# Attention heads of a graph network: small VectorE work given to ScalarE and GpSimd, and the causal mask added in the eviction

## The chip, the cores and the metric

The kernel is one program on one core of one Trainium2 chip. The metric is the device time of an execution in microseconds, lower is better; the number quoted is the median of several executions.

## What is computed

Two layers on 3327 nodes of 256 features. Layer 0 is a graph convolution and a mixture of experts, layer 1 a graph attention and then a causal multi-head attention with four query "experts" for each of four heads. Only that last part, the heads, is touched. The reference, cut to it (x is first layer-normalised):

```python
sx = einsum('bsh,ndh->bnsd', x, hl_w) + hl_b          # 4 heads of 64
pad = sx == 0
q = einsum('bnsd,neod->bneso', sx, wq)                # 4 experts a head
k = einsum('bnsd,nod->bnso', sx, wk)
v = einsum('bnsd,nod->bnso', sx, wv)
scores = einsum('bnesd,bntd->bnest', q, k) * d ** 0.5 + causal   # 0 or -inf above the diagonal
att = softmax(scores)
qkv = where(pad, 0, einsum('bnest,bntd->bnesd', att, v))
gs = softmax(out @ gate_w + gate_b)                   # out: qkv, experts side by side
hn = layernorm(sum over experts of qkv * gs + sx)     # over 64, with gain and bias
fx = hn, heads side by side;  pm = fx == 0
hx = relu(where(pm, 0, fx @ fc1 + fc1_b))
hx = layernorm(where(pm, 0, hx @ fc2 + fc2_b) + fx)
out = hx * softmax(hx @ fgate_w) by head              # added to x
```

## The kernel before

The rows stand in 26 tiles of 128. `heads` (L869) works through 104 units, a unit being one tile t and one head h (L1363), and each unit's keys are cut into t // 4 + 1 chunks of up to 512 (`span`, L1008); there are 392 chunks (L1364). For one chunk there are these steps:

- `fill` (L1015): TensorE makes the scores of the four experts, two products at a time in the upper and the lower half of the rows, into four PSUM banks. In the last chunk of a unit (`last`) each bank gets two more bf16 products, `own` times `after` (L1030 to L1036), that add -1e30 above the diagonal: eight products in all.
- `drain` (L1038): VectorE evicts each of the four banks to `sc` in SBUF with one instruction that also takes the row maximum into `mx` (L1046). After the last chunk the maxima are reduced to `nmax`.
- `weigh` (L1058): ScalarE takes Exp of the four parts with the maximum as bias and adds up the row sums.
- `turn` (L1079): VectorE transposes the weights in blocks of 32 x 32, in place.
- `attend` (L1091): TensorE multiplies the turned weights by the values `vr` into `po`.
- `over` (L1110) and `back` (L1120), once a unit: ScalarE copies `po` to `ot`, GpSimd multiplies it by the pad mask `sxd`, TensorE turns it back with the gate products (`ptO`), ScalarE copies that out.

Beside these run two kinds of generators, which do one step each time `run` (L1000) is called. `prepare` (L916), one for each tile, normalises the rows of the next tile, makes `sxt` (the sx of the reference, transposed), values, keys and queries; `sxd` is `sxt` in another layout, loaded by four DMAs on SP's queue, and compared with zero on VectorE (L994). `tail` (L1185), one for each tile but the last, does all from the gate softmax to the output, with `softmax4` (L1148) and `norm4` (L1166). The last tile has its own `last_tail` (L1262).

The order on each engine is the order of the program: `InOrder` (L50) chains each engine's instructions, so an engine that waits holds all behind it. The main loop (L1411 to L1433) drains some chunks ahead (`wanted`, L1397: all of a unit's maxima must be there before its first Exp), attends chunk k, turns chunk k + 1, asks for the values of chunk k + 2 on SP, does half of its Exp, calls `back` and `over` where a unit ended, gives the generators one step (after tile 7 not in the chunk that follows a unit's end, L1426), does the other half of Exp, and fills the next chunk. All products but `po` share one pool of four PSUM banks (`ps`, L881), score chunks and small work alike. `empty` (L892) sends an eviction to ScalarE or VectorE, whichever has the smaller sum in `load`; the amounts added to `load` are the author's costs. The constants of this stage are loaded and made by `heads_fixed` (L777) during the graph stage before it.

Nearly all instructions show line L61 in the profile, that of the recording helper, so groups are told apart by the names of their tiles.

Of the kernel before, what the change touches and what calls it, by code (L numbers as in the profile page):

```python
# [12 lines left out]
F32 = mybir.dt.float32  # L13
# [88 lines left out]
class Net:  # L102
# [674 lines left out]
    def heads_fixed(self, one, nc):  # L777


        a = self.a  # L780

        def load(src, shape, name):
            t = one.tile(shape, F32, name=name)
            nc.sync.dma_start(out=t, in_=src)
            return t

        def load_rows(src, n, name):
            return load(src.partition_broadcast(P), [P, n], name)
# [53 lines left out]
        own = [one.tile([P, P], BF16, name=f"own{k}") for k in range(2)]  # L842
        after = [one.tile([P, P], BF16, name=f"after{k}") for k in range(2)]

        def where(t, op, base, sign=1):

            for k in range(2):
                r = t[ds(64 * k, 64), :]
                nc.gpsimd.affine_select(
                    out=r, in_=r, compare_op=op, fill=0.0, base=base,  # L850
                    pattern=[[sign, P]], channel_multiplier=-2 * sign,
                )

        for k in range(2):
            yield
            nc.gpsimd.memset(own[k], 1.0)
            nc.gpsimd.memset(after[k], NEG)
        for made in (
            (own[0], ALU.is_ge, 0), (own[0], ALU.is_ge, 1, -1), (after[0], ALU.is_ge, -2),
            (own[1], ALU.is_equal, 0), (after[1], ALU.is_equal, -1),  # L860
        ):
            yield
            where(*made)
        self.fixed = (
            hlt, hlb, wv, gb, lng, lnb, fc1, fb1, fc2, fb2, fng, fnb, fgw, wk, wq, igw, own, after
        )


    def heads(self, xs, vs, out):  # L869
# [3 lines left out]
        with ExitStack() as ctx:  # L873
# [9 lines left out]
            hlt, hlb, wv, gb, lng, lnb, fc1, fb1, fc2, fb2, fng, fnb, fgw, wk, wq, igw, own, after = (  # L883
# [28 lines left out]

            def prepare(t, res):  # L916
# [10 lines left out]
                nc.gpsimd.tensor_tensor(rs, rs, self.nhalf[:, :1], ALU.pow)  # L927
                load["dve"] += 0.7
                yield
                xn = self.work.tile([P, D], F32, tag="xn", name="xn2", bufs=1)  # L930
                nc.vector.tensor_scalar(xn, x, mv[:, 0:1], rs, ALU.subtract, ALU.mult)
                load["dve"] += 0.35
# [11 lines left out]
                for c in range(2):  # L944
                    nc.scalar.activation(
                        sxt[:, c, :], pp[:, c, :], AF.Identity, bias=hlb[:, c : c + 1]
                    )
                load["act"] += 0.6
# [3 lines left out]
                for k in range(2):  # L952
                    for s in range(2):
                        nc.sync.dma_start(
                            out=sxd[ds(64 * k, 64), s::2, :], in_=sxt[ds(64 * s, 64), :, :]
                        )
# [37 lines left out]
                nc.vector.tensor_scalar(sxd, sxd, 0.0, None, ALU.not_equal)  # L994
                load["dve"] += 0.4
# [19 lines left out]
            def fill(u, g):  # L1015
# [4 lines left out]
                last = g == t // 4  # L1020
                pq = u["pq"] = []
                for i in range(2):
                    pq += [ps.tile([P, BLK], F32, tag="b", name="pqk") for _ in range(2)]
                    for k in range(2):
# [3 lines left out]
                            start=True, stop=not last,  # L1028
                        )
                    for m in range(2 if last else 0):  # L1030
                        for k in range(2):
                            r = ds(64 * k, 64)
                            nc.tensor.matmul(
                                pq[2 * i + k][:, n - P : n], own[m][r, :], after[m][r, :],
                                start=False, stop=(m == 1),
                            )  # L1036

            def drain(u, g):  # L1038

                n = span(u["t"], g)[1] * P  # L1040
                if g == 0:
# [3 lines left out]
                for e in range(4):  # L1045
                    nc.vector.tensor_scalar(  # L1046
                        sc[:, e, :n], u["pq"][e][:, :n], 1.0, None,
                        ALU.mult, ALU.max, accum_out=u["mx"][:, e, g : g + 1],
                    )
                    load["dve"] += 0.12 + 0.00104 * n  # L1050
                if g == u["t"] // 4:
# [6 lines left out]
            def weigh(u, g, experts):  # L1058
# [3 lines left out]
                if u["h"] == g == 0 and 0 in experts:  # L1062
                    q["den"] = sm.tile([P, 16, 7], F32, tag="den", name="aden", bufs=3)
# [15 lines left out]
            def turn(u, g):  # L1079
# [5 lines left out]
                load["dve"] += 0.1 + 0.00417 * n  # L1085

# [33 lines left out]
            def back(u):  # L1120
# [4 lines left out]
                if h == 0:  # L1125
                    r["qkv"] = tl.tile([P, 4, 4, 64], F32, tag="qkv", name="qkv", bufs=2)
                    r["glp"] = sm.tile([P, 4, 4, 4], F32, tag="glp", name="glp")
# [20 lines left out]
            def softmax4(g, n, tag):  # L1148
# [12 lines left out]
                nc.vector.tensor_tensor(s3, s3, m.unsqueeze(2).to_broadcast([P, n, 4]), ALU.mult)  # L1161
                load["dve"] += 0.6
# [3 lines left out]
            def norm4(v, g, b, tag):  # L1166

                mv = sm.tile([P, 4, 2], F32, tag=tag + "mv", name=tag + "mv")
                for h in range(4):
                    st = sm.tile([P, 6], F32, tag=tag + "st", name=tag + "st")  # L1170
                    nc.vector.bn_stats(st, v[:, ts(h, 64)])
                    nc.vector.bn_aggr(mv[:, h, :], st)
                rs = sm.tile([P, 4], F32, tag=tag + "rs", name=tag + "rs")
                nc.vector.tensor_scalar(
                    rs, mv.rearrange("p h s -> p s h")[:, 1, :], 1e-8, None, ALU.add
                )
                load["dve"] += 1.1
                nc.gpsimd.tensor_tensor(rs, rs, self.nhalf[:, :4], ALU.pow)
                v3 = v.rearrange("p (h d) -> p h d", h=4)
                nc.gpsimd.tensor_tensor(v3, v3, mv[:, :, 0:1].to_broadcast([P, 4, 64]), ALU.subtract)  # L1180
# [4 lines left out]
            def tail(t, sx, qkv, glp, den):  # L1185
# [16 lines left out]
                nc.vector.tensor_tensor(gs, gs, rd, ALU.mult)  # L1202
# [13 lines left out]
                norm4(fx, lng, lnb, "l1")  # L1216
# [3 lines left out]
                turned(fx, fxt)  # L1220
                yield
                h1 = tl.tile([P, 2, P], F32, tag="h1", name="h1")
# [6 lines left out]
                nc.vector.scalar_tensor_tensor(h1, fxt, 0.0, h1, ALU.not_equal, ALU.mult)  # L1229
                load["dve"] += 0.4  # L1230
                yield
                p2 = ps.tile([P, D], F32, tag="b", name="ph2")
                for c in range(2):
                    nc.tensor.matmul(p2[:, ts(c, P)], h1[:, c, :], fc2, start=True, stop=True)
                fo = tl.tile([P, D], F32, tag="fo", name="fo", bufs=3)
                nc.vector.tensor_tensor(
                    fo.rearrange("p (h d) -> p h d", h=4),
                    p2.rearrange("p (h d) -> p h d", h=4), rows(fb2), ALU.add,
                )
                nc.vector.scalar_tensor_tensor(fo, fx, 0.0, fo, ALU.not_equal, ALU.mult)  # L1240
                load["dve"] += 0.8
# [3 lines left out]
                norm4(fo, fng, fnb, "l2")  # L1245
# [4 lines left out]
                x = tl.tile([P, D], F32, tag="xend", name="xend", bufs=2)  # L1250
# [11 lines left out]
            def last_tail(t, c, sx, r):  # L1262
# [4 lines left out]
                if c == 0:  # L1267
# [3 lines left out]
                    x = r["x"] = tl.tile([P, D], F32, tag="xend", name="xend", bufs=2)  # L1271
# [45 lines left out]
                gs = yield from softmax4(gl, 2, "lgs")  # L1317
# [17 lines left out]
                h1 = tl.tile([P, P], F32, tag="h1", name="h1")  # L1335
# [21 lines left out]
                fg = yield from softmax4(pg, 1, "fg")  # L1357
# [632 lines left out]
```

## Time and profile before

| | us |
|---|---|
| median of three runs | 3050.26 |
| lowest, highest | 3046.64, 3051.62 |
| the profiled execution | 3033.66 |
| its span, first to last instruction | 3032.0 |
| first score product (start of the heads) | about 985 |
| VectorE busy in the span | 2506.5 |
| TensorE busy in the span | 2702.8 |
| ScalarE busy in the span | 1678.2 |
| GpSimd busy in the span | 886.5 |

The profile is one execution. A group's row gives the engine, the operation, output and input tiles with their shapes, the count, then the busy time and the mean duration, then the time the engine idled just before these instructions and what ended it. Matmul durations overlap and their ends are modelled. In a table of stretches the columns are span, then busy time (and number of instructions) of TensorE, its weight loads, VectorE, ScalarE and GpSimd, then the granted TensorE clock, the DMA share and GB/s. In a list of waits a row says who waited for whom: total, times and longest.

### The profile page before, as it was taken

The numbers are of one execution on the slowest core, as the hardware profiler recorded it, in microseconds if no ns is written. First come the engines' busy times: TensorE is split into PE (matmuls) and PEld (weight loads), VectorE is DVE, ScalarE is ACT, GpSimd is POOL, SyncE is SP. The second block draws the span as 40 slices with busy tenths as digits, with TensorE's granted clock in tenths as the row PEclk, the third lists the DMA queues.
The fourth block names the chain that finished last, engine by engine and source line by source line (L and its number), as shares of the span: only waits on it lengthen the run. The fifth ranks groups of instructions, "written<-read, shape, count | busy, mean of one in ns | idle before, by whom it ended". The sixth has DMA issues, their size and how long they took to land.

```text
span 3032.0 us, 126726 instructions
## 1 busy us (share of the span) xinstructions
PE 2702.8 (89%) x54254; PEld 2004.2 (66%) x54254; DVE 2506.5 (83%) x6203; ACT 1678.2 (55%) x4570; POOL 886.5 (29%) x1178
## 2 busy tenths in 40 slices
PE   7999988788899789998999998899989999999885
PEld 6878877667677666666666666666656666666554
DVE  5103643789997689999999999999999999999996
ACT  6410144555554556565666665666656666566664
POOL 6441644711322254432332221222121111111121
PEclk9999999889999889999999999999999999999998
DMA  9994578567773223333333343333333433433332
GB/s 376 356 314 134 190 240 261 199 212 253 247 266 99 67 74 110 95 95 104 111 99 106 104 120 105 99 111 105 111 107 104 116 107 114 116 111 106 113 106 74
DMA packets 258194, 449.81 MB, mean 148 GB/s; under 512 B 58816, under 2 KB 156608, under 8 KB 257504
## 3 DMA queue, kind: packets, MB, share of 16 engines
q1 hardware_dynamic: 245536, 417.50, 44.6%
q0 software_dynamic: 6576, 18.02, 1.6%
q8 instruction: 428, 7.01, 1.0%
q10 hardware_dynamic: 5520, 6.18, 0.6%
q14 instruction: 134, 1.10, 0.1%
HBM read 393.37 MB, written 25.88 MB: 138 GB/s over the span
## 4 chain that ended last, share of the span: by engine, by line
DVE 48%; PE 19%; issue 2%; ACT 1%; DMA 0%; POOL 0%; SPq 0%; DVEq 0%; POOLq 0%; ACTq 0%
DVE sc L61 40%; PE po L61 7%; PE pqk L61 6%; PE acc L61 2%; PE ptO L61 1%; DVE fo L61 1%; DVE l2mv L61 1%; DVE l1mv L61 1%; ACT sc L61 0%; PE pq L61 0%; DVE anmax L61 0%; DVE gl L61 0%; DVE l2st L61 0%; PE psxt L61 0%; DVE l1st L61 0%
## 5 line engine op out<-in xcount | busy, mean ns | idle before, releaser
L61 ACT ACTIVATE sc<-sc,anmax 128x512 f32<-128x512 f32 (+3 forms) x1568 | 1041.1, 670 | 124.1 <-DVE anmax L61 123.9
L61 DVE TENSOR_SCALAR_CACHE_REDUCE sc<-pqk 128x512 f32<-128x512 f32 (+3 forms) x1568 | 897.9, 626 | 52.8 <-PE pqk L61 50.9
L61 PEld LDWEIGHTS po<-sc,vr 32*64 32x64 f32 x43728 | 666.0, 131 | 337.7 <-DVE sc L61 195.5
L61 PE MATMUL po<-sc,vr 32*64 32x128 f32 x43728 | 769.2, 276 | 117.2 <-DVE sc L61 74.2
L61 PE MATMUL pqk<-kt,qt 64*128 64x512 f32 (+3 forms) x3136 | 800.4, 581 | 44.6 <-DVE sc L61 17.1
L61 DVE STREAM_TRANSPOSE sc<-sc 128x2048 f32<-128x2048 f32 (+3 forms) x392 | 816.1, 2082 | 12.9 <-ACT sc L61 12.9
L61 PEld LDWEIGHTS pqk<-kt,qt 64*128 64x128 f32 x3136 | 314.4, 187 | 232.4 <-issue 80.0
L61 PE MATMUL acc<-wh,p 128*128 128x259 f32 x1352 | 310.0, 387 | 34.6 <-DVE p L61 34.5
L61 PEld LDWEIGHTS acc<-wh,p 128*128 128x128 f32 x1352 | 254.2, 191 | 92.7 <-DVE p L61 51.9
L61 PE MATMUL acc<-y,pan 128*128 128x256 f32 x1352 | 301.3, 382 | 11.9 <-DMA pan<-in_adjt_dram 10.2
L61 POOL TENSOR_TENSOR ot<-ot,sxd 128x512 f32<-128x512 f32 x103 | 131.7, 1279 | 611.1 <-ACT ot L61 600.8
L61 ACT ACTIVATION_READ_ACCUMULATOR sc<-sc,anmax 128x1 f32 x1568 | 302.1, 193 | 0.0
L61 PEld LDWEIGHTS acc<-y,pan 128*128 128x128 f32 x1352 | 256.0, 191 | 52.2 <-issue 17.5
L61 ACT ACTIVATE u<-u,d 128x512 f32<-128x512 f32 (+1 forms) x182 | 125.1, 688 | 159.5 <-DVE u L61 159.3
L61 ACT COPY qkv<-ptO 128x256 f32<-128x256 f32 x104 | 38.7, 373 | 222.9 <-PE ptO L61 222.9
L61 DVE SCALAR_TENSOR_TENSOR u<-bc,d 128x512 f32<-128x512 f32 (+1 forms) x182 | 135.8, 747 | 0.1
L61 DVE SCALAR_TENSOR_TENSOR p<-pan,u 128x512 f32<-128x512 f32 (+1 forms) x182 | 126.4, 694 | 10.0 <-PE acc L61 5.7
L61 PE MATMUL ptO<-igw,ot 128*128 128x68 f32 x832 | 116.4, 284 | 15.6 <-DVE sc L61 11.6
L61 DVE DVE_READ_ACCUMULATOR sc<-pqk 128x1 f32 x1568 | 128.6, 82 | 0.0
L61 PEld LDWEIGHTS ptO<-igw,ot 128*128 128x128 f32 x832 | 102.3, 193 | 34.8 <-issue 20.9
L61 ACT ACTIVATE junk<-ar 128x1664 bf16<-128x1664 f32 x52 | 82.7, 1591 | 66.7 <-DMA ar<-in_adj_dram 65.4
L61 PEld LDWEIGHTS <-own 64*128 64x128 bf16 x832 | 53.7, 95 | 94.5 <-issue 82.9
(324 smaller groups left out, 2872.5 us busy)
## 6 DMA issues: line engine op xcount, KB each, us to landing
vr<-vs SPq DMA_DIRECT2D x976, 128.0 KB, 2.6
ar<-in_adj_dram SPq DMA_DIRECT2D x104, 832.0 KB, 7.8
vr<-vs SPq DMA_DIRECT2D x544, 96.0 KB, 2.2
pan<-in_adjt_dram SPq DMA_DIRECT2D x156, 256.0 KB, 4.7
pan<-in_adjt_dram SPq DMA_DIRECT2D x26, 1024.0 KB, 10.7
pan<-in_adjt_dram SPq DMA_DIRECT2D x20, 832.0 KB, 4.7
w1e<-w SPq DMA_DIRECT2D x59, 256.0 KB, 2.5
took<-places SPq DMA_DIRECT2D x59, 129.0 KB, 5.0
```

What stands on the lines that cost most here:

```text
L61: made = make(*args, **kw)
```

## The change

Five things are done, all in the heads.

The mask: the `own` and `after` products are gone. A tile `mask` of 128 x 512 holds zeros, with -1e30 above the diagonal in its last 128 columns; in a unit's last chunk the eviction adds its last n columns to the scores and takes the maximum in the same instruction.

The layer norms of the tail: `norm4` took the statistics of four heads with four pairs of VectorE instructions and a fifth. It becomes a generator: one reduction on VectorE gives minus the sums, ScalarE squares 64 x + ns with an accumulated sum, GpSimd scales both; four `run` steps are added to a tail in all.

The zero tests: `nonzero` is Sign and then Square on ScalarE. It replaces the comparisons for `sxd` (tested before the DMAs), `h1` and `fo`; the products with them go to GpSimd, as does the bias of `fo`, whose eviction goes through `empty`.

`prepare`'s normalisation of `xn` goes from one VectorE instruction to two on GpSimd, and three small products of the softmaxes go to GpSimd.

Buffers: `den` from 3 to 2, `glp` from 4 to 3, `h1` and `xend` from 2 to 1; the last tile's `xend` load is made in its second half.

```diff
+        mask = one.tile([P, BLK], F32, name="mask")
+        yield
+        nc.gpsimd.memset(mask, 0.0)
+        yield
+        nc.gpsimd.affine_select(
+            out=mask[:, BLK - P :], in_=mask[:, BLK - P :], compare_op=ALU.is_ge, fill=NEG, base=0,
+            pattern=[[-1, P]], channel_multiplier=1,
+        )
...
+            def nonzero(dst, src):
+                nc.scalar.activation(dst, src, AF.Sign)
+                nc.scalar.activation(dst, dst, AF.Square)
+                load["act"] += 0.75
...
# prepare
-                nc.vector.tensor_scalar(xn, x, mv[:, 0:1], rs, ALU.subtract, ALU.mult)
-                load["dve"] += 0.35
+                nc.gpsimd.tensor_tensor(xn, x, mv[:, 0:1].to_broadcast([P, D]), ALU.subtract)
+                nc.gpsimd.tensor_tensor(xn, xn, rs.to_broadcast([P, D]), ALU.mult)
...
+                nz = self.work.tile([P, 2, P], F32, tag="xn", name="nz", bufs=1)
+                nonzero(nz, sxt)
...
-                            out=sxd[ds(64 * k, 64), s::2, :], in_=sxt[ds(64 * s, 64), :, :]
+                            out=sxd[ds(64 * k, 64), s::2, :], in_=nz[ds(64 * s, 64), :, :]
...
-                nc.vector.tensor_scalar(sxd, sxd, 0.0, None, ALU.not_equal)
-                load["dve"] += 0.4
...
# fill
-                            start=True, stop=not last,
+                            start=True, stop=True,
-                    for m in range(2 if last else 0):
-                        for k in range(2):
-                            r = ds(64 * k, 64)
-                            nc.tensor.matmul(
-                                pq[2 * i + k][:, n - P : n], own[m][r, :], after[m][r, :],
-                                start=False, stop=(m == 1),
-                            )
...
# drain
+                    if last:
+                        nc.vector.tensor_tensor_reduce(
+                            sc[:, e, :n], s, mask[:, BLK - n :], 1.0, NEG, ALU.add, ALU.max, m
+                        )
+                    else:
+                        nc.vector.tensor_scalar(
+                            sc[:, e, :n], s, 1.0, None, ALU.mult, ALU.max, accum_out=m
+                        )
...
# softmax4
-                nc.vector.tensor_tensor(s3, s3, m.unsqueeze(2).to_broadcast([P, n, 4]), ALU.mult)
-                load["dve"] += 0.6
+                (nc.vector if last else nc.gpsimd).tensor_tensor(
+                    s3, s3, m.unsqueeze(2).to_broadcast([P, n, 4]), ALU.mult
+                )
+                load["dve"] += 0.4
...
# norm4
-                for h in range(4):
-                    st = sm.tile([P, 6], F32, tag=tag + "st", name=tag + "st")
-                    nc.vector.bn_stats(st, v[:, ts(h, 64)])
-                    nc.vector.bn_aggr(mv[:, h, :], st)
-                rs = sm.tile([P, 4], F32, tag=tag + "rs", name=tag + "rs")
-                nc.vector.tensor_scalar(
-                    rs, mv.rearrange("p h s -> p s h")[:, 1, :], 1e-8, None, ALU.add
-                )
-                load["dve"] += 1.1
+                nc.vector.tensor_reduce(ns, v3, AX.X, ALU.add, negate=True)
+                load["dve"] += 0.35
+                yield
+                rs = sm.tile([P, 4], F32, tag=tag + "rs", name=tag + "rs")
+                for h in range(4):
+                    nc.scalar.activation(
+                        sq, v[:, ts(h, 64)], AF.Square, bias=ns[:, h : h + 1], scale=64.0,
+                        accum_out=rs[:, h : h + 1],
+                    )
+                load["act"] += 1.2
+                yield
+                nc.gpsimd.tensor_scalar(ns, ns, 1 / 64, None, ALU.mult)
+                nc.gpsimd.tensor_scalar(rs, rs, 1 / 64**3, 1e-8, ALU.mult, ALU.add)
                 nc.gpsimd.tensor_tensor(rs, rs, self.nhalf[:, :4], ALU.pow)
-                nc.gpsimd.tensor_tensor(v3, v3, mv[:, :, 0:1].to_broadcast([P, 4, 64]), ALU.subtract)
+                nc.gpsimd.tensor_tensor(v3, v3, ns.unsqueeze(2).to_broadcast([P, 4, 64]), ALU.add)
...
# tail
-                nc.vector.tensor_tensor(gs, gs, rd, ALU.mult)
+                nc.gpsimd.tensor_tensor(gs, gs, rd, ALU.mult)
...
+                nz = tl.tile([P, 2, D], F32, tag="nzf", name="nzf", bufs=1)
+                nonzero(nz[:, 0, :], fx)
+                yield
+                nonzero(nz[:, 1, :], fxt.rearrange("p c q -> p (c q)"))
...
-                nc.vector.scalar_tensor_tensor(h1, fxt, 0.0, h1, ALU.not_equal, ALU.mult)
-                load["dve"] += 0.4
+                nc.gpsimd.tensor_tensor(
+                    h1, h1, nz[:, 1, :].rearrange("p (c q) -> p c q", c=2), ALU.mult
+                )
...
-                nc.vector.tensor_tensor(
-                    fo.rearrange("p (h d) -> p h d", h=4),
-                    p2.rearrange("p (h d) -> p h d", h=4), rows(fb2), ALU.add,
-                )
-                nc.vector.scalar_tensor_tensor(fo, fx, 0.0, fo, ALU.not_equal, ALU.mult)
-                load["dve"] += 0.8
+                empty(fo, p2, D)
+                f3 = fo.rearrange("p (h d) -> p h d", h=4)
+                nc.gpsimd.tensor_tensor(f3, f3, rows(fb2), ALU.add)
+                nc.gpsimd.tensor_tensor(fo, fo, nz[:, 0, :], ALU.mult)
                 nc.gpsimd.tensor_tensor(fo, fo, fx, ALU.add)
```

More of the change, by code (lines that the diff above doesn't have):

```diff
@@ L837, in heads_fixed @@
                 )
-        own = [one.tile([P, P], BF16, name=f"own{k}") for k in range(2)]
-        after = [one.tile([P, P], BF16, name=f"after{k}") for k in range(2)]
-        def where(t, op, base, sign=1):
-            for k in range(2):
[L848 to L851, printed above, removed]
-                )
[L854 to L863, printed above, removed]
+        mask = one.tile([P, BLK], F32, name="mask")
[6 more added lines that the diff above has]
+        )
         self.fixed = (
-            hlt, hlb, wv, gb, lng, lnb, fc1, fb1, fc2, fb2, fng, fnb, fgw, wk, wq, igw, own, after
+            hlt, hlb, wv, gb, lng, lnb, fc1, fb1, fc2, fb2, fng, fnb, fgw, wk, wq, igw, mask
         )
@@ L881, in heads @@
             ps = ctx.enter_context(tc.tile_pool(name="psm", bufs=4, space=PSUM))
-            hlt, hlb, wv, gb, lng, lnb, fc1, fb1, fc2, fb2, fng, fnb, fgw, wk, wq, igw, own, after = (
+            hlt, hlb, wv, gb, lng, lnb, fc1, fb1, fc2, fb2, fng, fnb, fgw, wk, wq, igw, mask = (
                 self.fixed
@@ L926, in prepare @@
                 nc.vector.tensor_scalar(rs, mv[:, 1:2], 1e-5, None, ALU.add)
-                nc.gpsimd.tensor_tensor(rs, rs, self.nhalf[:, :1], ALU.pow)
                 load["dve"] += 0.7
                 yield
+                nc.gpsimd.tensor_tensor(rs, rs, self.nhalf[:, :1], ALU.pow)
                 xn = self.work.tile([P, D], F32, tag="xn", name="xn2", bufs=1)
-                nc.vector.tensor_scalar(xn, x, mv[:, 0:1], rs, ALU.subtract, ALU.mult)
-                load["dve"] += 0.35
+                nc.gpsimd.tensor_tensor(xn, x, mv[:, 0:1].to_broadcast([P, D]), ALU.subtract)
+                nc.gpsimd.tensor_tensor(xn, xn, rs.to_broadcast([P, D]), ALU.mult)
                 yield
@@ L1019, in fill @@
                 n *= P
-                last = g == t // 4
                 pq = u["pq"] = []
@@ L1027, in fill @@
                             pq[2 * i + k][:, :n], u["qt"][r, h, i, :], kt[r, h, ds(lo * P, n)],
-                            start=True, stop=not last,
+                            start=True, stop=True,
                         )
-                    for m in range(2 if last else 0):
-                        for k in range(2):
-                            r = ds(64 * k, 64)
-                            nc.tensor.matmul(
-                                pq[2 * i + k][:, n - P : n], own[m][r, :], after[m][r, :],
-                                start=False, stop=(m == 1),
-                            )
             def drain(u, g):
                 n = span(u["t"], g)[1] * P
+                last = g == u["t"] // 4
                 if g == 0:
@@ L1045, in drain @@
                 for e in range(4):
-                    nc.vector.tensor_scalar(
-                        sc[:, e, :n], u["pq"][e][:, :n], 1.0, None,
-                        ALU.mult, ALU.max, accum_out=u["mx"][:, e, g : g + 1],
-                    )
+                    s, m = u["pq"][e][:, :n], u["mx"][:, e, g : g + 1]
+                    if last:
[6 more added lines that the diff above has]
+                        )
                     load["dve"] += 0.12 + 0.00104 * n
-                if g == u["t"] // 4:
+                if last:
                     u["nmax"] = sm.tile([P, 4], F32, tag="nmax", name="anmax")
@@ L1062, in weigh @@
                 if u["h"] == g == 0 and 0 in experts:
-                    q["den"] = sm.tile([P, 16, 7], F32, tag="den", name="aden", bufs=3)
+                    q["den"] = sm.tile([P, 16, 7], F32, tag="den", name="aden", bufs=2)
                 for k in experts:
@@ L1085, in turn @@
                 load["dve"] += 0.1 + 0.00417 * n
+            sq = one.tile([P, 64], F32, name="sq")
             po = ps_o.tile([P, 4, BLK], F32, tag="po", name="po")
@@ L1126, in back @@
                     r["qkv"] = tl.tile([P, 4, 4, 64], F32, tag="qkv", name="qkv", bufs=2)
-                    r["glp"] = sm.tile([P, 4, 4, 4], F32, tag="glp", name="glp")
+                    r["glp"] = sm.tile([P, 4, 4, 4], F32, tag="glp", name="glp", bufs=3)
                 pt = ps.tile([P, 4, 68], F32, tag="b", name="ptO")
@@ L1146, in rows, with softmax4 @@
                 return v.unsqueeze(1).to_broadcast([P, 4, 64])
-            def softmax4(g, n, tag):
+            def softmax4(g, n, tag, last=False):
                 g3 = g.rearrange("p (n e) -> p n e", e=4)
@@ L1166, in norm4 @@
             def norm4(v, g, b, tag):
-                mv = sm.tile([P, 4, 2], F32, tag=tag + "mv", name=tag + "mv")
-                for h in range(4):
-                    st = sm.tile([P, 6], F32, tag=tag + "st", name=tag + "st")
-                    nc.vector.bn_stats(st, v[:, ts(h, 64)])
-                    nc.vector.bn_aggr(mv[:, h, :], st)
-                rs = sm.tile([P, 4], F32, tag=tag + "rs", name=tag + "rs")
-                nc.vector.tensor_scalar(
-                    rs, mv.rearrange("p h s -> p s h")[:, 1, :], 1e-8, None, ALU.add
-                )
-                load["dve"] += 1.1
+                v3 = v.rearrange("p (h d) -> p h d", h=4)
+                ns = sm.tile([P, 4], F32, tag=tag + "ns", name=tag + "ns")
+                nc.vector.tensor_reduce(ns, v3, AX.X, ALU.add, negate=True)
+                load["dve"] += 0.35
+                yield
+                rs = sm.tile([P, 4], F32, tag=tag + "rs", name=tag + "rs")
+                for h in range(4):
+                    nc.scalar.activation(
[6 more added lines that the diff above has]
+                nc.gpsimd.tensor_scalar(rs, rs, 1 / 64**3, 1e-8, ALU.mult, ALU.add)
                 nc.gpsimd.tensor_tensor(rs, rs, self.nhalf[:, :4], ALU.pow)
-                v3 = v.rearrange("p (h d) -> p h d", h=4)
-                nc.gpsimd.tensor_tensor(v3, v3, mv[:, :, 0:1].to_broadcast([P, 4, 64]), ALU.subtract)
+                nc.gpsimd.tensor_tensor(v3, v3, ns.unsqueeze(2).to_broadcast([P, 4, 64]), ALU.add)
                 nc.gpsimd.tensor_tensor(v3, v3, rs.unsqueeze(2).to_broadcast([P, 4, 64]), ALU.mult)
@@ L1215, in tail @@
                 yield
-                norm4(fx, lng, lnb, "l1")
+                yield from norm4(fx, lng, lnb, "l1")
                 yield
@@ L1220, in tail @@
                 turned(fx, fxt)
+                nz = tl.tile([P, 2, D], F32, tag="nzf", name="nzf", bufs=1)
+                nonzero(nz[:, 0, :], fx)
                 yield
-                h1 = tl.tile([P, 2, P], F32, tag="h1", name="h1")
+                nonzero(nz[:, 1, :], fxt.rearrange("p c q -> p (c q)"))
+                h1 = tl.tile([P, 2, P], F32, tag="h1", name="h1", bufs=1)
                 ph = ps.tile([P, 2, P], F32, tag="b", name="ph1")
@@ L1235, in tail @@
                 fo = tl.tile([P, D], F32, tag="fo", name="fo", bufs=3)
-                nc.vector.tensor_tensor(
-                    fo.rearrange("p (h d) -> p h d", h=4),
-                    p2.rearrange("p (h d) -> p h d", h=4), rows(fb2), ALU.add,
-                )
-                nc.vector.scalar_tensor_tensor(fo, fx, 0.0, fo, ALU.not_equal, ALU.mult)
-                load["dve"] += 0.8
+                empty(fo, p2, D)
+                f3 = fo.rearrange("p (h d) -> p h d", h=4)
+                nc.gpsimd.tensor_tensor(f3, f3, rows(fb2), ALU.add)
+                nc.gpsimd.tensor_tensor(fo, fo, nz[:, 0, :], ALU.mult)
                 nc.gpsimd.tensor_tensor(fo, fo, fx, ALU.add)
@@ L1244, in tail @@
                 yield
-                norm4(fo, fng, fnb, "l2")
+                yield from norm4(fo, fng, fnb, "l2")
                 yield
@@ L1249, in tail @@
                 turned(fo, fot)
-                x = tl.tile([P, D], F32, tag="xend", name="xend", bufs=2)
+                x = tl.tile([P, D], F32, tag="xend", name="xend", bufs=1)
                 nc.sync.dma_start(out=x, in_=xs[ts(t, P), :])
@@ L1270, in last_tail @@
                     r["fot"] = tl.tile([P, 2, P], F32, tag="fotl", name="fotl", bufs=1)
-                    x = r["x"] = tl.tile([P, D], F32, tag="xend", name="xend", bufs=2)
+                else:
+                    x = r["x"] = tl.tile([P, D], F32, tag="xend", name="xend", bufs=1)
                     nc.sync.dma_start(out=x, in_=xs[ts(t, P), :])
@@ L1316, in last_tail @@
                 nc.vector.tensor_tensor(gl, gl, gb[:, ds(8 * c, 8)], ALU.add)
-                gs = yield from softmax4(gl, 2, "lgs")
+                gs = yield from softmax4(gl, 2, "lgs", True)
                 nc.vector.tensor_tensor(gs, gs, rd, ALU.mult)
@@ L1334, in last_tail @@
                 nc.tensor.matmul(ph, fc1, fxt, start=True, stop=True)
-                h1 = tl.tile([P, P], F32, tag="h1", name="h1")
+                h1 = tl.tile([P, P], F32, tag="h1", name="h1", bufs=1)
                 nc.scalar.activation(h1, ph, AF.Relu, bias=fb1)
@@ L1356, in last_tail @@
                     nc.tensor.matmul(pg, fot[:, k, :], fgw[:, k, :], start=(k == 0), stop=(k == 1))
-                fg = yield from softmax4(pg, 1, "fg")
+                fg = yield from softmax4(pg, 1, "fg", True)
                 f3 = fo.rearrange("p (h d) -> p h d", h=4)
```

## The prediction

> **What bounds the kernel now.** First the page's busy shares and slices: the change touches only the last stage, which begins near 985 us (the first score products) and is two thirds of the span. From there VectorE stands at 9 tenths nearly throughout, and TensorE hardly lower.
>
> ```profile
> PE 2702.8 (89%) x54254; PEld 2004.2 (66%) x54254; DVE 2506.5 (83%) x6203; ACT 1678.2 (55%) x4570; POOL 886.5 (29%) x1178
> ...
> PE   7999988788899789998999998899989999999885
> ...
> DVE  5103643789997689999999999999999999999996
> ```
>
> Then the stage cut in three (tiles 0 to 7; 8 to 24; the last tile), with busy time by engine, and what VectorE waited for in it.
>
> ```profile
> 985.00:1290.00 305.00, 268.75 (x5554) 198.87 (x5561) 251.94 (x783) 177.58 (x582) 136.80 (x149) 0.92 0.31 86
> 1290.00:2878.00 1588.00, 1449.55 (x40845) 988.86 (x40837) 1529.96 (x3676) 999.26 (x2980) 344.15 (x383) 0.99 0.37 108
> ...
> DVE sc L61 <- PE pqk L61: 50.9, 67, 3.5
> DVE sxd L61 <- DMA sxd<-sxt: 14.6, 3, 6.9
> DVE sc L61 <- ACT sc L61: 12.9, 12, 3.3
> ```
>
> The columns are span, then PE, weight loads, VectorE, ScalarE, GpSimd. In the long middle part VectorE is busy 1530 of 1588 us (96%), TensorE 1450 (91%), ScalarE 63%, GpSimd 22%. VectorE is the bound, TensorE 80 us behind it: that distance decides the forecast. Waits of VectorE for score products are 51 us in all; they are the price of the two engines handing four PSUM banks to each other.
>
> Third, the groups by shape in this stage: what a chunk must have, and what the change takes away.
>
> ```profile
> L61 DVE TENSOR_SCALAR_CACHE_REDUCE sc<-pqk 128x512 f32<-128x512 f32 x976 | 613.1, 682 | 36.3 <-PE pqk L61 35.1
> L61 DVE STREAM_TRANSPOSE sc<-sc 128x2048 f32<-128x2048 f32 x244 | 562.4, 2305 | 9.3 <-ACT sc L61 9.3
> ...
> L61 DVE SCALAR_TENSOR_TENSOR fo<-fx,fo 128x256 f32<-128x256 f32 x25 | 12.4, 494 | 1.8
> L61 DVE TENSOR_SCALAR sxd<-sxd 128x512 f32<-128x512 f32 x26 | 12.2, 468 | 14.6 <-DMA sxd<-sxt 14.6
> L61 DVE TENSOR_SCALAR xn<-xres,pmv,prs 128x256 f32<-128x256 f32 x25 | 12.1, 486 | 1.9 <-POOL prs L61 1.9
> ...
> L61 DVE SCALAR_TENSOR_TENSOR h<-fxt,h 128x256 f32<-128x256 f32 x25 | 11.5, 460 | 0.0
> ```
>
> Last, the timeline of VectorE, because durations overlap and starts do not:
>
> ```profile
> 2532.96 0.68 DVE L61 TENSOR_SCALAR_CACHE_REDUCE sc<-pqk 128x512 f32<-128x512 f32 x1
> 2533.57 0.08 DVE L61 DVE_READ_ACCUMULATOR sc<-pqk 128x1 f32 x1
> ...
> 2539.59 0.19 DVE L61 BATCH_NORM_STATS2 l1st<-fx 128x6 f32<-128x64 f32 x1
> 2539.81 0.18 DVE L61 BATCH_NORM_AGGREGATE l1mv<-l1st 128x2 f32<-128x6 f32 x1
> ...
> 2541.01 0.17 DVE L61 TENSOR_SCALAR l1rs<-l1mv 128x4 f32<-128x4 f32 x1
> 2541.08 0.68 DVE L61 TENSOR_SCALAR_CACHE_REDUCE sc<-pqk 128x512 f32<-128x512 f32 x1
> ```
>
> An eviction of 512 columns is 0.68 long, but the next starts 0.61 later: an operation occupies VectorE for its duration less about 0.07. One norm4 occupies it from 2539.59 to 2541.08, 1.49 us, more than two evictions.
>
> [...] the one two-input operation with an accumulator and a PSUM source, sq<-gram,ident (128 columns), took 290 ns[...]. The changed kernel's built program has five table loads, as before, so Sign and Square bring none.
>
> **The change part by part.** Per tile (25 or 26 of each), VectorE's occupied time:
> - two norm4: 2 x 1.49 go, 2 reductions of 256 to 4 come. Nearest rows: gsm<-gl, 16 columns, 170 ns; gl<-glp, 64 columns, 269. [...] at the slope between the two (2.06), 660. I take 0.42 less 0.07, 0.35. Saved 2 x 1.14 = 2.28 (at worst 1.8).
> - fo: bias and mask, 2568.46 to 2569.30 in the timeline: 0.84; the copy that replaces them goes to ScalarE in 24 of 25 cases (built program).
> - h 0.46, sxd 0.47, xn 0.49, each less 0.07: 1.21.
> - three softmax products (278, 175 and 178 ns) less overlap: about 0.5.
>
> Sum 4.8 a tile, 123 us over 25.5. Against it: the load counters now send 16 more evictions to VectorE (thirteen of 256 columns at 0.35, three of 512 at 0.62): 6 us. And the 416 masked evictions, which the trace does not show. A custom operation with two inputs is there, sg<-sg,dst of 1664 columns, 1.88 us[...]. Bounds: equal to the eviction now (0.61 apart), or as u<-bc,d (two inputs, 0.67 apart)[...]. I take +0.03, 12 us (0 to 25). Net VectorE: 123 - 6 - 12 = 105 us.
>
> TensorE loses 832 bf16 products. They keep it busy 76.5 us, but overlap fp32 products: a fill with them took from 2557.85 to 2560.12, one without them 1.99, so 0.28 x 104 = 29 us. I take 29 (up to 76).
>
> ScalarE gains per tile eight Squares of 64 (from the Exp rows, 715, 608, 513 and 394 ns for 512 to 128, about 340 each), six Sign/Square of 256 at about 0.30 and a copy: 4.9, some 125 us, on 1259 of 2047: about 70%. GpSimd gains xn 2 x 0.62, three products of 256 at 0.73, seven small ones at some 0.4 (nearest is the power of one column, 0.56): 6.2 a tile, 160 us on 507: about 34%. I cost both at nothing, for the cover: a chunk lasts 4.65 us with 2.8 us of Exp, leaving ScalarE 1.8 against at most 1.4 of Squares in a step; GpSimd's steps have two chunks (9.3 us) before TensorE or VectorE asks for fx or fo, and the longest becomes 5.5. If that cover fails, the queues behind are in order: GpSimd's ot product stands behind a tail's work, TensorE's ptO waits for it, and the next fill behind that. The four sxd loads on SP now wait for nz, two ScalarE operations (0.6 us) later, and vr loads stand behind them; vr is asked for two chunks ahead (9 us) and lands in 2.6, so nothing. The tail gets four more steps, 21; the last whole tail has 24 before the end, so the end isn't moved. The last tile's x load comes later but long before its use. The set-up on GpSimd shrinks beside the graph stage: nothing.
>
> Where it goes: in tiles 8 to 24, VectorE's work becomes 1530 - 17 x 4.8 + 17 x 0.5 + 3 = 1460 us, TensorE's 1450 - 17 x 4 x 0.28 = 1431. Before, the stage lasted 58 us more than VectorE's work. With the engines now 29 apart, not 80, I let that grow to 75: 1535, so 53 saved. Tiles 0 to 7: VectorE is at 83% and TensorE at 88%, so of 39 us of removed work I count a third, and some of the 14.6 us wait of sxd, 14 together. Last tile: its own tail is unchanged, one whole tail runs in it: 3. Sum 70 us. On the profiled execution (3033.66, span 3032.0) this gives 2964. That execution was 16.6 below the median of the runs shown, 3050.26; I take the same 70 from the median: 2980.
>
> **Rivals.**
> - VectorE remains the only bound: all 105 us come, and the sxd wait of 15: 2930. For it: VectorE's waits for products are only 51 us. Against: TensorE's 1431.
> - TensorE takes over, or longer chains make it wait in order for GpSimd: in the middle part its 1431 plus its present 138 us of idle is 1569, a gain of 19, some 30 to 35 with the ends: 3017. For it: its idle time before po and pqk is put down to VectorE's sc, but an engine of 91% has little to give. Against: those very waits shorten.
> - Slower: the masked eviction runs at half rate[...]. Each then costs 0.53 more, 416 x 0.53 = 222, on a gain of 82 without it: 3190. From 0.20 us more each there is no gain. [...]
>
> **How the numbers follow.** Forecast 0.55, whole gain 0.20, TensorE bound 0.17, half rate or late queues 0.05, no difference 0.03. Faster by over 0.2% (6 us, about what a measurement of this kernel can tell): 0.92; same 0.03; slower 0.05. The range reaches into both faster rivals, 2935 to 3022; half of the whole-gain case and the last two are left out, 0.18.
>
> **What would show it.** Right: norm4 as one reduction of some 0.4 us; masked evictions 0.61 to 0.67 apart; VectorE still over 93% in tiles 8 to 24, its waits for pqk up to some 70 us, a chunk without small work still 4.65 us. Wrong: masked evictions over 0.8 apart; ptO, ph or pt waiting for GpSimd more than 20 us in all; TensorE busier than VectorE.

## The result

| | us |
|---|---|
| before, median of 4 runs (3037.82 to 3051.62) | 3048.45 |
| changed, median of 4 runs (2994.64 to 3002.89) | 3001.88 |
| ratio, 95% interval | 0.9848, 0.9819 to 0.9877 |
| changed, profiled execution | 3002.89 |
| its span | 3000.9 |

The change makes the kernel faster by 47 us, inside the range and below the 70 that were forecast. Between the two profiled executions it is 31 us, because that of the kernel before, at 3033.66, lay 15 us under its median.

First the stage cut as before, at the first transposes of tiles 8 and 25. The page of the changed kernel, and its three stretches (span; then busy time of TensorE, its weight loads, VectorE, ScalarE, GpSimd; granted clock near the end):

```profile
PE 2668.5 (89%) x53422; PEld 1968.9 (66%) x53422; DVE 2398.4 (80%) x5617; ACT 1818.6 (61%) x5131; POOL 998.2 (33%) x1468
...
DVE  5102643689999565788999999999999999999997
```

```profile
985.00:1330.70 345.70, 281.93 (x5378) 203.38 (x5378) 230.52 (x645) 213.00 (x723) 162.01 (x220) 0.87 0.28 77
1330.70:2853.90 1523.20, 1409.33 (x40256) 955.29 (x40255) 1448.52 (x3257) 1101.82 (x3384) 431.07 (x602) 1.00 0.39 112
2853.90:3001.00 147.10, 108.16 (x3522) 76.17 (x3513) 124.50 (x282) 86.35 (x262) 30.06 (x43) 0.92 0.32 93
```

And the kernel before, cut at the same events:

```profile
985.00:1290.70 305.70, 269.44 (x5603) 199.57 (x5610) 252.64 (x787) 178.28 (x584) 136.80 (x149) 0.92 0.31 86
1290.70:2878.50 1587.80, 1449.35 (x40822) 988.65 (x40808) 1529.76 (x3676) 999.03 (x2978) 344.15 (x383) 0.99 0.37 108
2878.50:3032.00 153.50, 111.50 (x3547) 77.55 (x3538) 127.80 (x304) 81.21 (x241) 26.41 (x33) 0.92 0.31 90
```

The middle stretch became 65 us shorter, the last 6 us shorter; the first became 40 us longer. (Its left edge is a fixed time. From the first transpose to that of tile 8 it was 302 us and is 336: 34 longer. The other 6 are the stage before the heads ending later, which varied by 9 us between the profiles of this study.) The digits of VectorE say the same: from the 14th slice on, where the heads start, 68999999 has become 56578899. In the first stretch VectorE has 22 us less to do and takes 40 longer.

What VectorE waited for in the middle, before and then after (who waited for whom: total, times, longest):

```profile
DVE sc L61 <- PE pqk L61: 37.1, 51, 3.5
DVE sc L61 <- ACT sc L61: 0.7, 2, 0.5
```

```profile
DVE sc L61 <- PE pqk L61: 55.7, 76, 2.5
DVE sc L61 <- ACT sc L61: 9.9, 15, 1.8
```

And in the first stretch of the changed kernel, VectorE's waits and TensorE's:

```profile
DVE sc L61 <- PE pqk L61: 40.0, 32, 5.7
DVE kt L61 <- PE pk L61: 18.4, 5, 9.0
DVE v L61 <- PE pv L61: 15.5, 3, 6.9
...
PE pt L61 <- POOL xn L61: 18.7, 4, 5.9
PE ptO L61 <- POOL ot L61: 14.5, 4, 6.6
```

VectorE waits for TensorE, and TensorE for GpSimd. In the kernel before, TensorE waited only 1.4 us for ot in this stretch, and VectorE still made xn. One such wait, first GpSimd and then TensorE, in tile 4:

```profile
1119.15 0.23 POOL L61 TENSOR_SCALAR l1ns<-l1ns 128x4 f32<-128x4 f32 x1
...
1122.92 0.73 POOL L61 TENSOR_TENSOR fx<-fx,lnb 128x256 f32<-128x256 f32 x1
1123.60 0.22 POOL L61 TENSOR_TENSOR gss<-gss,gsm 128x16 f32<-128x16 f32 x1
...
1128.32 0.72 POOL L61 TENSOR_TENSOR fx<-fx,sx 128x256 f32<-128x256 f32 x1
1129.00 1.26 POOL L61 TENSOR_TENSOR ot<-ot,sxd 128x512 f32<-128x512 f32 x1
...
1130.31 0.91 PE L61 MATMUL ptO<-igw,ot 128*128 128x68 f32 x3 [6.63 <-POOL ot L61]
```

ScalarE had finished the copy of ot at 1121.30 (0.60 from 1120.70). GpSimd was then in norm4 of one tail (4.5 us) and went on to the gate product of another (5.4 us); ot came after both, at 1129.00. TensorE stood 6.63 us before ptO, and the next fill stands behind ptO.

### The profile page after: what moved, and what is told of

Its sections match the earlier page's. It is cut to its first block, busy times and chain, and to the rows that moved or that the text cites. A ratio compares the mean times of both kernels' runs of the same rounds, so it can differ in the third digit from the quotient of the medians.

```text
span 3000.9 us, 125355 instructions
## 1 busy us (share of the span) xinstructions
PE 2668.5 (89%) x53422; PEld 1968.9 (66%) x53422; DVE 2398.4 (80%) x5617; ACT 1818.6 (61%) x5131; POOL 998.2 (33%) x1468
## 5 line engine op out<-in xcount | busy, mean ns | idle before, releaser
L61 PE MATMUL pqk<-kt,qt 64*128 64x512 f32 (+3 forms) x3136 | 781.1, 583 | 21.6 <-DVE sc L61 4.4
L61 DVE TENSOR_SCALAR_CACHE_REDUCE sc<-pqk 128x512 f32<-128x512 f32 (+2 forms) x1152 | 655.8, 623 | 68.0 <-PE pqk L61 66.2
L61 DVE CUSTOM_DVE_ANT_0 sc<-pqk,mask 128x512 f32<-128x512 f32 (+3 forms) x416 | 242.0, 636 | 30.2 <-PE pqk L61 29.8
L61 DVE CUSTOM_DVE_ANT_0 sg<-sg,dst 128x1664 bf16<-128x1664 bf16 (+2 forms) x56 | 100.0, 1794 | 1.2 <-ACT dst L61 1.0
```

The lines of the kernel that those rows point to most:

```text
L61: made = make(*args, **kw)
```

## The experiments

All but e4 have the mask in the eviction. Each was compared with runs of the kernel before on the same chip. The chips differ from group to group: the kernel before had medians of 3042.2 us beside e1 to e4, 3041.3 beside e5 to e8, 3044.6 beside e9 to e11, and 3048.5 beside the change. So a few us between the medians of different groups are not to be read, and the parts of the change are told apart by the stretches. These are from one profile each, between the first transposes of tiles 0, 8 and 25.

| | median us | ratio to before, 95% | tiles 0-7 | tiles 8-24 |
|---|---|---|---|---|
| before | 3041.3 to 3048.5 | 1 | 302 | 1588 |
| the change | 3001.9 | 0.9848 (0.9819 to 0.9877) | 336 | 1523 |
| e1 early tiles old, one wait too many | 2989.8 | 0.9811 (0.9797 to 0.9825) | 320 | 1529 |
| e2 evictions placed as before | 3003.6 | 0.9862 (0.9846 to 0.9879) | 335 | 1522 |
| e3 mask alone | 3040.2 | 0.9992 (0.9980 to 1.0004) | 300 | 1593 |
| e4 moved work alone | 3008.8 | 0.9881 (0.9865 to 0.9898) | 334 | 1526 |
| e5 early tiles old | 2972.4 | 0.9770 (0.9753 to 0.9787) | 298 | 1527 |
| e6 early prepare old | 2990.2 | 0.9834 (0.9814 to 0.9855) | 326 | 1523 |
| e7 early tail old | 2980.1 | 0.9792 (0.9776 to 0.9809) | 311 | 1529 |
| e8 more VectorE work | 3042.9 | 1.0009 (0.9997 to 1.0021) | 339 | 1564 |
| e9 early prepare and norm4 old | 2968.0 | 0.9756 (0.9736 to 0.9775) | 306 | 1526 |
| e10 early norm4 moved | 2982.4 | 0.9798 (0.9781 to 0.9815) | 314 | 1522 |
| e11 early norm4 in one step | 2999.8 | 0.9845 (0.9825 to 0.9865) | 317 | 1537 |

**e1_early_old and e5_early_fixed: the moved work, but not in tiles 0 to 7.** The theory after the result was that the moved work stands in series with TensorE there. The rivals were that the clock fell by itself and that the mask hurts units of one chunk.

```diff
+            EARLY = 8
# e.g. in prepare, and so for norm4, h1, fo, sxd and the softmax products
+                if t < EARLY:
+                    nc.vector.tensor_scalar(xn, x, mv[:, 0:1], rs, ALU.subtract, ALU.mult)
+                else:
                     nc.gpsimd.tensor_tensor(xn, x, mv[:, 0:1].to_broadcast([P, D]), ALU.subtract)
                     nc.gpsimd.tensor_tensor(xn, xn, rs.to_broadcast([P, D]), ALU.mult)
```

> The changed kernel, but tiles 0 to 7 keep the old forms of the small work on VectorE (norm4, xn, the zero tests, fo's bias, the softmax products); the mask in the eviction stays everywhere. Theory (in tiles 0 to 7 the moved work is in series: GpSimd is late, TensorE waits in order behind it, VectorE waits for TensorE): the 34 us that tiles 0 to 7 lost come back, 2965 to 2975 us, tiles 0 to 7 in about 300 us, TensorE's waits for GpSimd under 10 us, clock there back at 0.9. Rival (tiles 0 to 7 were slow because the granted clock fell from 0.92 to 0.85 by itself): clock still 0.85 and 2995 to 3003. Rival (the mask is what hurts in short units, where every chunk is a last chunk): 2990 to 3003.

Measured: 2989.83, between the theory and the rivals. Its profile shows why: the power for xn was still issued in the step of xn itself, as in the changed kernel, so that VectorE now waited for GpSimd.

```profile
DVE xn L61 <- POOL prs L61: 17.8, 6, 4.5
```

e5 also issues that power a step earlier in these tiles.

```diff
+                if t < EARLY:
+                    nc.gpsimd.tensor_tensor(rs, rs, self.nhalf[:, :1], ALU.pow)
                 yield
```

> As e1, but for tiles 0 to 7 GpSimd's power for xn is issued one step earlier too, as in the kernel before (in e1 VectorE waited 17.8 us for it, 6 times). Theory (moved work in series in tiles 0 to 7): that wait goes, 2970 to 2978 us, tiles 0 to 7 in 300 to 306 us, and TensorE's half-clock stretches there fall from 95 to about 65 us[...]. Rival (clock falls by itself): 2985 to 2992 as e1.

Measured: 2972.43, tiles 0 to 7 in 298 us. The loss of tiles 0 to 7 is gone, and the middle keeps its gain. In the stretches of e5 (edges at its own tiles 8 and 25) the first is 311 us, not 346, and VectorE does 253 us of work in it, as before the change:

```profile
985.00:1296.20 311.20, 271.50 (x5370) 198.38 (x5375) 252.88 (x786) 180.94 (x592) 137.29 (x150) 0.90 0.31 86
1296.20:2823.40 1527.20, 1406.89 (x40280) 955.49 (x40269) 1455.77 (x3290) 1093.24 (x3348) 420.58 (x578) 1.00 0.39 112
```

The clock of the first stretch was 0.92 before, 0.87 with the change and 0.90 here. The time at half clock between the first transposes of tiles 0 and 8, added up from the trace's clock records, was 51, 85 and 52 us; in e1, with its one wait too many, it was 82. (From 985 to 1330 us it was 51, 92 and 65, so the 65 expected of e5 came.) So the clock did not fall by itself: in e5, which has the rest of the change, the added slow time was gone with the waits. One stretch at half clock falls into the wait shown above: TensorE stood from 1123.69 to 1130.31, and the changed kernel's trace has the clock at 1.00 from 1121.2 to 1128.0 and at 0.50 from 1128.0 to 1134.8. How the wait and the slower clock hang together was not shown, and what the slower clock added to the loss was not separated. It is hardly the larger part: 34 us more (85 less 51) at half clock lose the work of 17 us (an estimate from these 34 us and the granted 0.50), half of the loss, and e9 below, with 72 us at half clock, takes only 4 us more for these tiles than the kernel before.

**e3_mask_only and e4_moves_only: the two halves of the change.**

```diff
# e3: kernel before, with mask, fill and drain of the changed kernel, den in 2 buffers
# e4: changed kernel, with own, after, fill and drain of the kernel before
```

> The kernel before with the mask alone changed (eviction with two inputs in the last chunk, no own products, den in 2 buffers). The masked eviction measured 0.014 us more between starts: 416 x 0.014 = 6 us more on VectorE, the bound; TensorE is relieved by 29 us. If VectorE alone counts: 3048 to 3056. If TensorE's relief counts as well, through VectorE's waits for products: 3030 to 3043.

Measured: 3040.24, a ratio of 0.9992 with 1 inside its interval: no difference. (The ranges above were counted from a slower median of the kernel before than the 3042.2 beside this run, so it falls into the second of them without a gain.) The masked eviction costs what the plain one does. Its group, and one row of four in the changed kernel's timeline:

```profile
L61 DVE TENSOR_SCALAR_CACHE_REDUCE sc<-pqk 128x512 f32<-128x512 f32 x656 | 411.9, 682 | 40.1 <-PE pqk L61 39.4
...
L61 DVE CUSTOM_DVE_ANT_0 sc<-pqk,mask 128x512 f32<-128x512 f32 x320 | 200.5, 681 | 19.0 <-PE pqk L61 18.7
```

```profile
2512.55 0.69 DVE L61 CUSTOM_DVE_ANT_0 sc<-pqk,mask 128x512 f32<-128x512 f32 x1
2513.16 0.08 DVE L61 DVE_READ_ACCUMULATOR2_ANT mx<- 128x1 f32 x1
2513.16 0.69 DVE L61 CUSTOM_DVE_ANT_0 sc<-pqk,mask 128x512 f32<-128x512 f32 x1
```

681 ns against 682, and 0.61 us from start to start, as for the plain one. (In the changed kernel the plain eviction of 512 columns took 133 ns more than that of 384, which took 549: 1.04 ns a column. At half the speed 512 columns would take 0.53 us more, an estimate from this slope. In the kernel before, sq<-gram,ident, with two inputs and an accumulator, had taken 290 ns for 128 columns, the plain eviction of 128 columns 285.) The rival of half rate is refuted. Relieving TensorE of 832 products gives nothing that this measurement tells.

> The changed kernel with the eight products of a last chunk put back and the plain eviction. If the relief of TensorE is worth something only once VectorE has less to do: 3015 to 3030, tiles 8 to 24 longer by 15 to 25 us than in the changed kernel. If VectorE alone is the bound there: 2995 to 3002. Tiles 0 to 7 lose in both.

Measured: 3008.77, between the two ranges; tiles 8 to 24 took 1526 us, 3 more than in the changed kernel, not 15 to 25. The intervals of e4 and the change overlap. So the gain is that of the moved work, and TensorE is not what the middle waits on.

**e8_more_sums: is VectorE still the bound in tiles 8 to 24?**

```diff
-                nc.vector.tensor_reduce(ns, v3, AX.X, ALU.add, negate=True)
+                for _ in range(1 + more):          # more = 3 from tile 8 on
+                    nc.vector.tensor_reduce(ns, v3, AX.X, ALU.add, negate=True)
```

> The changed kernel; in tiles 8 to 25 norm4's reduction on VectorE is made four times in place of once (same result), 6 more a tile of 0.33 to 0.36 us, some 2.1 us a tile, 36 us over tiles 8 to 24. If VectorE is still the bound there: 3030 to 3040. If TensorE or the handing over of banks has become the bound: 3002 to 3018.

Measured: 3042.92, a little above the range for VectorE as the bound; in the middle

```profile
1331.40:2895.20 1563.80, 1431.45 (x40255) 967.22 (x40254) 1487.95 (x3353) 1101.71 (x3384) 431.02 (x602) 0.99 0.38 110
```

against 1523.20 and 1448.52 in the changed kernel: 39.4 us more work of VectorE, 40.6 more of time. All of it lies on the path: VectorE is still the bound there.

**e2_evict_as_before: the evictions that the load counters sent to VectorE.**

```diff
# nonzero, norm4
-                load["act"] += 0.75
...
-                load["act"] += 1.2
# and the amounts for VectorE as in the kernel before (1.1 for norm4, 0.35 for xn, ...)
```

> The changed kernel, but the load counters get the amounts that they got before, so that all small evictions go to the engines that had them before (four on VectorE, not 20). Theory: VectorE's in-order waits for these evictions in tiles 0 to 3 (50 us for kt, v, qt, sx, xt) are a share of the loss, 10 to 15 us: 2985 to 2992. If GpSimd's lateness is all of it and the evictions only wait along with it: 2998 to 3003. If ScalarE is the short engine there: over 3005.

Measured: 3003.55. VectorE's waits for kt, v, sx, qt and xt, 50 us in the changed kernel, were no cause: they fell to 27 us, yet tiles 0 to 7 still took 335 us. VectorE waited for the next scores in their place, 68.6 us where it had been 40.0:

```profile
DVE sc L61 <- PE pqk L61: 68.6, 33, 11.8
```

**e6_early_prep, e7_early_tail: which part of the moved work.** In e6 only `prepare` has its old form in tiles 0 to 7 (the power a step earlier with it), in e7 only `tail`.

> The changed kernel; in tiles 0 to 7 only prepare keeps its old form (xn and the zero test for sxd on VectorE, the power a step earlier), the tail's work is moved as in the change. Of the loss of tiles 0 to 7: if xn behind GpSimd's tail work is the larger part (TensorE waited 18.7 us for xn), 2982 to 2990; if the tail's work is (ot behind it: 14.5 us, and ScalarE's), 2993 to 3001.

Measured: 2990.21, at the edge of the range for xn; tiles 0 to 7 in 326 us.

> The mirror of e6: in tiles 0 to 7 the tail keeps its old forms on VectorE, prepare is as changed (xn on GpSimd, Sign and Square before sxd). If the tail's work is the larger part: 2978 to 2987; if xn is: 2990 to 3000. Together e6 and e7 should give back what e5 does.

Measured: 2980.08 and 311 us. The tail is the larger part: of the 38 us by which e5 shortens tiles 0 to 7 (336 to 298), its old forms win back 25, those of prepare 10. The medians put them in the same order. In e6 TensorE's wait for ot stays and that for xn has gone from 18.7 to 3.9; in e7 xn stays and no wait of ptO for GpSimd is among the longer ones:

```profile
PE ptO L61 <- POOL ot L61: 14.8, 5, 6.6
...
PE pt L61 <- POOL xn L61: 3.9, 1, 3.9
```

```profile
PE pt L61 <- POOL xn L61: 14.6, 5, 4.2
```

**e9_norm_old, e10_norm_moved, e11_norm_one_step: which part of the tail.** All have the old `prepare` in tiles 0 to 7. In e9 norm4 is old too and the rest of the tail is moved, in e10 only norm4 is moved, and e11 is e6 with norm4 in one step:

```diff
                 load["dve"] += 0.35
-                yield
+                if not early:
+                    yield
...
                 load["act"] += 1.2
-                yield
+                if not early:
+                    yield
```

> As e6 (prepare in its old form in tiles 0 to 7), and there norm4 in its old form as well: five instruction kinds on VectorE, no extra steps; the rest of the tail's work stays on GpSimd and ScalarE. e6 measured 2990, e5 (all old in these tiles) 2972. If norm4, with its four more steps, its eight Squares and its two more GpSimd operations, is what the tail loses by: 2972 to 2980. If the zero tests, bias and softmax products behind one another on GpSimd are: 2984 to 2991.

Measured: 2968.04, below both ranges; tiles 0 to 7 in 306 us.

> The mirror of e9: in tiles 0 to 7 all is old but norm4, which is split over VectorE, ScalarE and GpSimd with its extra steps. If norm4 is the cause: 2984 to 2991; if the rest is: 2972 to 2980.

Measured: 2982.44, between the two ranges; tiles 0 to 7 in 314 us. Its TensorE waited 11.5 us for ot, that of e9 2.9. From e5 to e6, which differ in the whole of the tail, tiles 0 to 7 grow by 28 us; norm4 alone adds 16 of them (e10), the rest of the tail alone 8 (e9). So norm4 is most of the tail's loss. How much of it comes through GpSimd and how much through the Squares on ScalarE was not separated; VectorE's waits for Exp before tile 8 had grown from 3.4 to 12.8 us with the change.

> As e6, but in tiles 0 to 7 the moved norm4 makes its three parts in one step, so that a tail has 17 steps again and not 21. If the loss comes from the longer tails (more of them open at once, forced on by the limit of four): 2975 to 2985. If it comes from the queues themselves: 2987 to 3000, as long as e6 or longer.

Measured: 2999.81; its interval overlaps that of e6. Tiles 0 to 7 took 317 us, 9 fewer than in e6, but tile 8 took 64 us and not 54, and tiles 0 to 9 together 442 against 438. With 17 steps for a tail in place of 21 the loss doesn't shrink, part of it only moves behind tile 7. That speaks against the longer tails as the cause, but doesn't exclude them, since e11 also packs the three engines' parts into one step: before tile 8 TensorE's wait for ot has shrunk (2.9 us), while VectorE's for scores is 37.3 us, against 28.3 in e6. Which wait starts these stays open.

e9 and e5 beat both kernels; their intervals overlap.

## Why the prediction was right, and where it failed

The forecast (2980, range 2935 to 3022) had the direction and, within 22 us, the time. Its sum was 53 + 14 + 3; between the two profiles it came out as 65 - 34 + 6, and 6 us less from the stage before. That the time fell inside the range owes something to luck: tiles 0 to 7 missed their forecast by 48 us, and the range reached that far only for a rival in which the middle gains little. A full gain in the middle with a loss before it was among none of the cases.

- *Bound by VectorE.* Right, and stronger than put: e8 shows that its extra work costs the whole amount of time, e4 that TensorE's products cost next to none there. In the middle I put VectorE's work after the change at 1460 us; it was 1449. Two terms were a little large: the new reduction takes 0.39 and 0.38 us (taken: 0.42, an estimate; the 170 ns of gsm<-gl and 240 columns more at 1.04 ns, the slope of the evictions, make the same), and the masked eviction costs nothing more (taken: +0.03, which is 8.5 us in the middle). So 81 us of VectorE's work left the middle, and 65 of them were gained.
- *What VectorE idles.* I let it grow from 58 to 75 us in the middle; it is 1523.2 - 1448.5 = 75. The size was right, my reason (TensorE's 1431 close behind; measured 1409) is not shown: with TensorE's products put back (e4) the stretch hardly grew. VectorE's waits for scores grew by 19 us, those for ScalarE's Exp, which now has Squares beside it, by 9; other gaps shrank. With tiles 0 to 7 the waits for scores came to 96 us, above the 70 that were set as a sign of being right.
- *TensorE loses 832 products, 29 us.* It lost 31 us of busy time in all (1830 to 1799 in the three stretches), 40 in the middle, where 19 had been counted, while it was busy 12 us longer in the first; and the time did not follow, as e4 shows: the rival "TensorE takes over" is refuted for the middle.
- *ScalarE and GpSimd cost nothing, for the cover.* Nearly right in tiles 8 to 24, and the step that failed in tiles 0 to 7. The cover was worked out for a chunk of 4.65 us and one tail at a time. Before tile 8 the generators get a step after every chunk and a tile has 4 or 8 chunks, against 21 steps of a tail, so several tails and a `prepare` issue to GpSimd in a row; in tile 4 it went 9.9 us without a pause before it reached ot. The text named this very chain and priced it at nothing. Several tails are open in tiles 8 to 11 too, with 8 steps to a tile, and yet TensorE's waits for xn and ot after tile 7 come to under 2 us; what spares these tiles was not tested. Of the amounts, ScalarE's was too small (it gained 143 us, not 125: a Sign or Square of 256 columns took 0.42 us, not 0.30) and GpSimd's too large (116 us, not 160).
- *Tiles 0 to 7 gain 14 us.* They lost 34. "A third of the removed work" was no reading of a view: VectorE was at 83% there and TensorE at 88%, neither full, so that less work on VectorE need not mean less time: what it idles counts as well, and in the first stretch that went from 53 to 115 us. VectorE's wait of 14.6 us for sxd went, as hoped, and longer ones for scores, kt and v came. The mark set for being wrong, TensorE waiting over 20 us for GpSimd, was met: 18.7 + 14.5 = 33 us.
- *No table loads, SP's order, the end.* As forecast: both traces have five table loads, the last stretch gave 6 us, not 3, and no new wait for vr or sxd stands out.

## What to carry to other kernels

Price moved work stage by stage: where one engine was nearly full (96%), 65 of the 81 us that left it were gained; where none was full (83 and 88%), the same move lengthened the waits and 34 us were lost. An engine with a low share of busy time is no free place if its queue is in order and something on the path waits in it (GpSimd was busy 162 of the 346 us of the first stretch, 47%, and TensorE waited 33 us for it): look at how much is issued to it in a row between two things that others wait for. A move can be kept for the stages that pay: with the old forms in tiles 0 to 7, the change was worth 2.3%, not 1.5%.

## What the runs showed of the hardware

Adding a mask tile from SBUF while evicting 512 scores from PSUM with a running maximum took 681 ns, the plain eviction 682. GpSimd's tiny operations are cheaper than I took them for (0.4 us): 0.19 and 0.23 us for a scaling of 128 x 4, 0.20 to 0.22 for products of 4 to 16 columns, while the power of 128 x 4 took 1.04. A Square of 64 columns with bias and sum took 0.35 us on ScalarE, and a read of its sum 0.19.
